# Two places for half sums in PSUM, another pattern of combined images from 126 to 145, and another order of the first steps, in a quantised 3x3 convolution after group normalisation

## The chip, the core and the metric

The kernel runs on one core of a Trainium2 chip. That core has five engines with a queue each, which run in order and meet only at semaphores: TensorE (PE, with its weight loads as PEld), VectorE (DVE), ScalarE (ACT), GpSimd (POOL), and SyncE (SP), which only issues DMAs here. Matmuls write to PSUM (8 banks of 128 partitions x 512 float32); DVE and ACT read it from there. The metric is the device time of one execution in microseconds; lower is better.

## What is computed

160 images of 128 channels and 32 x 32 pixels are normalised in groups of four channels, and convolved with 3x3 weights that are quantised to a two-part grid (a step s1 and a fifth of it, s2); the convolution is added to the image. Image i goes with weight set i // 32 of five in the kernel's order of images (the kernel takes the images set by set).

```python
def _L0_conv_ref(x, U):                    # N = 5 sets of weights, K = 3, PAD = 1
    beta = jnp.max(U)
    alpha = jnp.min(U)
    s1 = (beta - alpha) / 3.0
    v1 = s1 * floor(U / s1)
    s2 = s1 / 5.0
    v2 = s2 * floor((U - v1) / s2)
    w = (v1 + v2).reshape(OUT_CH * N, IN_CH, K, K)
    xb = x.reshape(B // N, N * C, H, W)
    act = conv_general_dilated(xb, w, strides 1, padding 1, feature_group_count=N)
    return act.reshape(B, C, H, W)
def _gn(v, G=32, eps=1e-5):                # mean and variance over (C // G, H, W)
    return (g - m) / jnp.sqrt(s + eps)
x = x + _L0_conv_ref(_gn(x), U)
```

## The kernel before

**Data.** Images are loaded two at a time into a ring of 11 places in SBUF (`load`), measured, normalised, convolved, added to and stored from there (`store`). The five sets of weights are quantised on DVE a column of the 3x3 taps at a time (`make_column`, some 13 DVE operations per column, handed out one by one by `take(later, 1)` between the images' work), turned by PE through PSUM (`turn_column`, tile `pt`) and kept by ACT and POOL (`keep_column`): for each column three taps (G), and three combinations of them for the half sums (SUM, DIFF, MINUS_G2).

**Statistics.** ACT reads each image twice (L194 sums, L201 squares); a few early images are measured by DVE instead (`BY_VECTOR`, with `bn_stats`, L184). For a group of 2, 4 or 8 images PE averages over channels (`means` L210, `variances` L227, tile `pg` in PSUM), ACT takes the result out (L219, L233), and POOL does the small arithmetic up to `rstd` and `shift` (L221 to L246). Groups end at images 2, 4, 8, 12, 16, 20, 24 and then every eight.

**Precision.** The normalised image is used as the sum of two float16 parts, high and low. An image that is not *combined* is normalised by ACT (`normalise`, z, L523), its high part cast by ACT (`high_part`, hi, L531), its low part made by DVE (`low_part`, lo, L589), and then combinations of the rows of lo alone by DVE (`combinations`, L603 to L606). Its high part goes through the nine taps directly (`taps`, L629: 18 matmuls of up to 512 columns); its low part goes through half sums.

**Half sums.** For a pair of output rows the vertical part of a 3x3 convolution is had from a sum and a difference of row pairs: PE makes m1 (SUM) and m2 (DIFF) of the half height in PSUM (`sums_of_pairs`), ACT copies m2 to SBUF (`leave`, L725), DVE writes m1+m2 and m1-m2 into the two banks of `eo` (`pairs`, L735 and L737), and PE adds the remaining terms into `eo` (`rest_of_column`). A *combined* image goes this way with both parts: POOL (`outer_rows`, L554, L555) and DVE (`combine`, L565 to L571) form the row combinations v of the raw image in float32, ACT scales and rounds them to vh (`high_combined`, L576), DVE makes vl (`low_combined`, L582). Before the change the odd images from 7 to 145 are combined, and from 146 on two of every three.

**Matmuls of an image.** Combined: 12 of 512 columns for the half sums and 24 of 256 in `rest_of_column`. Not combined: 6 of 512, 18 of 512 (taps) and 12 of 256.

**Order.** All is written out by hand in `run` (a manual schedule: each engine gets its instructions in the order of the program). In iteration i, `conv(i)` puts on PE the half sums of image i+1 and then the rest of image i; the other engines get, in this order: the low part of i+2; measuring, first half; taking image i-1 out of `eo` (`residual`: ACT L754 with a later adding DMA by POOL, L773; every eighth image, the first and the last ones by DVE, L765); the border rows of i+4; `leave(i+1)`; the high part of i+3; measuring, second half; `pairs(i+1)` on DVE; `combine(i+4)`, or a step of quantisation. The first three images are not combined and take both parts through the taps; image 2 uses the two banks of m1 and m2 as its output.

**PSUM.** Two `eo` of two banks each (`ps_eo`), one bank each for m1 and m2 (`ps_m`), one for the statistics (`ps_stat`), and one for turned weights and the range of the weights (`ps_tr`): eight.

Of the kernel before, what the change touches and what calls it, by code (L numbers as in the profile page):

```python
# [19 lines left out]
ROW = 3  # L20
# [139 lines left out]
class Statistics:  # L160
# [5 lines left out]
    def __init__(self, nc, small, psum, gavg, mhalf, nb, scale, name):  # L166
        self.nc, self.small, self.psum, self.gavg, self.mhalf = nc, small, psum, gavg, mhalf
        self.nb, self.scale, self.name = nb, scale, name

        self.mv = self.tile("mv", [nb, 2])  # L170
# [35 lines left out]
    def means(self):  # L206
        self.pg = self.psum.tile(
            [self.nc.NUM_PARTITIONS, 2, self.nb], F32, tag="pg", name=f"pg{self.name}"
        )
        self.nc.tensor.matmul(  # L210
            self.pg[:, 0, :], self.gavg, self.mv[:, :, 0], start=True, stop=True
        )
# [36 lines left out]
def general_path(tc, keep, steps, x, u, out):  # L249
# [8 lines left out]
    with tc.If(far > 0), ExitStack() as ctx:  # L258
# [9 lines left out]
        for n in range(N_SETS):  # L268
# [11 lines left out]
            with tc.For_i(0, IMGS // N_SETS, 1) as b:  # L280
                xt = one.tile([P, H * W], F32, tag="xt", name=f"g_xt{n}")
                nc.sync.dma_start(xt, xv[n, :, bass.ds(b, 1), :])
                stats = Statistics(nc, one, psum, gavg, mhalf, 1, 1.0, f"g{n}")
                stats.image(0, xt)
                stats.means()
# [26 lines left out]
class Main:  # L312
# [27 lines left out]
    BY_VECTOR = (8, 10, 11, 14, 19, 24, 29, 34)  # L340
    THIRDS = 146
# [7 lines left out]
    def __init__(self, tc, ctx, keep, x, u, out):  # L349
# [9 lines left out]
        def pool(name, bufs, **kw):  # L359
# [18 lines left out]
        self.ps_stat = pool("ps_stat", 1, space=PSUM)  # L378
        self.ps_tr = pool("ps_tr", 1, space=PSUM)
        self.steps = Steps(nc, keep)  # L380

        self.pair = [
            ps_m.tile([P, self.H // 2, self.W], F32, tag=name, name=name) for name in ("m1", "m2")
        ]
# [52 lines left out]
    def over_partitions(self, ext1, ident, between):  # L437


        nc, P = self.nc, self.P  # L440
        rows = self.ps_tr.tile([1, 2, P], F32, tag="pt", name="rows")
        for k in range(2):
            nc.tensor.transpose(rows[:, k, :], ext1[:, k : k + 1], ident)
        between()
        top = self.const.tile([1, 2], F32, tag="top", name="top")
        nc.vector.tensor_reduce(top, rows, AX.X, ALU.max)
        spread = self.ps_tr.tile([P, 2], F32, tag="pt", name="spread")
        nc.tensor.matmul(spread, self.ones, top, start=True, stop=True)
        return spread

    def make_column(self, n, col, by_scalar=False):

        nc, P = self.nc, self.P
        un = self.us[n].rearrange("o i (r c) -> o i r c", c=ROW)[:, :, :, col]
        k1, k2 = yield from self.steps.quantise(self.qpool, un, f"{n}_{col}", MM, by_scalar)
        if n == 0:
            parts = ((k1, self.ident5), (k2, self.ident))
            self.keep_column(n, col, self.turn_column(n, col, parts))  # L460
        else:
            m = self.qpool.tile([P, P, ROW], MM, tag="m", name=f"m{n}_{col}")
            nc.vector.scalar_tensor_tensor(m, k1, 5.0, k2, ALU.mult, ALU.add)
            self.columns.append((n, col, ((m, self.ident),)))
            yield

    def turn_column(self, n, col, parts):
        nc, P = self.nc, self.P
        pt = self.ps_tr.tile([P, ROW, P], F32, tag="pt", name=f"pt{n}_{col}")
# [6 lines left out]
        return pt  # L476

    def keep_column(self, n, col, pt):


        nc, P = self.nc, self.P
        wt = self.wpool.tile([P, 6, P], MM, tag=f"wt{col}", name=f"wt{n}_{col}")
        half = self.qpool.tile([P, ROW, P], MM, tag="half", name=f"half{n}_{col}")
        outer = self.qpool.tile([P, P], MM, tag="outer", name=f"outer{n}_{col}")
        nc.scalar.mul(wt[:, self.G, :], pt, 2.0 / LIFT)  # L485
        nc.scalar.mul(half, pt, 1.0 / LIFT)
# [4 lines left out]
        self.wts[n, col] = wt  # L491
# [5 lines left out]
    def stats_of(self, k):  # L497
        if k not in self.stats:
            self.stats[k] = Statistics(
                self.nc, self.small, self.ps_stat, self.gavg, self.mhalf, len(self.groups[k]),  # L500
                self.steps.lift, k,
            )
        return self.stats[k]
# [24 lines left out]

    def high_part(self, i):
# [4 lines left out]
    def combined(self, i):  # L534

        if i < self.STEADY or i >= self.imgs:
            return False

        return i % 2 == 1 if i < self.THIRDS else i % 3 != 1

# [135 lines left out]

    def both(self, i):
# [3 lines left out]
    def sums_of_pairs(self, i):  # L681

        both = self.both(i)
        for a, kind in ((1, self.DIFF), (0, self.SUM)):
            for col in self.COLS:
                for j, (_, st) in enumerate(both):
                    self.product(
                        self.pair[a], i, kind, st[:, a], col,
# [33 lines left out]
    def leave(self, i):  # L722

        m2 = self.evac.tile([self.P, self.H // 2, self.W], F32, tag="m2", name=f"m2_{i}")
        self.nc.scalar.copy(m2, self.pair[1])  # L725
        self.m2[i] = m2

    def pairs(self, i, between=lambda: None):
# [3 lines left out]
        m1, m2 = self.pair[0], self.m2.pop(i)  # L732
# [49 lines left out]
    def run(self):  # L782
# [44 lines left out]
        spread = self.over_partitions(ext1, ident, self.stats_of(0).means)  # L827
# [31 lines left out]
        self.stats[1].means()  # L859
# [8 lines left out]
        run(first)  # L868
        self.warm_up(2)
# [15 lines left out]
        run(second)  # L885
        measure(1, 5)
# [8 lines left out]
        self.stats[2].means()  # L895
        self.stats[2].deviations()
        self.low_part(3)
# [4 lines left out]
        for i in range(self.imgs):  # L902
# [3 lines left out]
            def on_the_way(col):  # L906
                if col == self.COLS[1]:
                    for st in ready:
                        st.means()
                    for *column, parts in self.columns:  # L910
                        turned.append((column, self.turn_column(*column, parts)))
# [32 lines left out]
            if i < self.FIRST:  # L944
# [5 lines left out]
                if i == 2:  # L950
# [4 lines left out]
                    self.pairs(3)  # L955
                    self.low_part(4)
                    run(self.combinations(4))
                self.residual(j)
                if i == 1:
                    measure(0, 11)  # L960
            else:
# [23 lines left out]
                if part:  # L985
                    self.normalise(i + 3)
# [11 lines left out]
            for column, pt in turned:  # L998
                self.keep_column(*column, pt)
            turned = []  # L1000

            if i >= self.FIRST:
# [5 lines left out]
                else:  # L1008
                    take(later, 1)
# [63 lines left out]
```

## Time and profile before

| | before |
|---|---|
| median of 4 runs (lowest to highest) | 991.56 us (991.36 to 991.73) |
| profiled execution: its own time | 991.84 us |
| its span, first to last instruction | 990.0 us |
| granted TensorE clock | 0.998 |

The page of the profile gives, for each engine, its busy time and share of the span, and the chain of work that ended last. Lines of a timeline give start (us from the span's start), duration, engine, source line, operation, output<-inputs, shape and how many in a row; in square brackets how long the engine was idle before and what ended that. Matmuls overlap in such lines (a row of 0.38 us is followed by the next start 0.216 us later), so PE's pace is read from starts, not from durations. Lines of waits give engine, line and tile, what it waited for, us in total, number and longest.

### The profile page before, as it was taken

What the parts mean: (1) busy time and instruction counts of PE and PEld (TensorE: products, weight loads), DVE (VectorE), ACT (ScalarE), POOL (GpSimd) and SP (SyncE); (2) the same over time, 40 slices, a digit from 0 to 9 for tenths busy, and PEclk for the clock granted to TensorE, in tenths of its full rate; (3) what the DMA queues carried; (4) which work ended last, traced back from release to release, by engine and by line L of the source; (5) the groups of instructions that cost most, each with busy time, mean ns of one, the idle gap of its engine ahead of it and who ended that gap; (6) DMA issues with size and microseconds to landing.
All of it is one profiled execution on the core that took longest, in us unless ns stands there. A gap on an engine that the chain in (4) does not pass through costs nothing.

```text
span 990.0 us, 16124 instructions
## 1 busy us (share of the span) xinstructions
PE 958.1 (97%) x5938; PEld 578.1 (58%) x5938; DVE 928.2 (94%) x1256; ACT 894.9 (90%) x1224; POOL 392.2 (40%) x565
## 2 busy tenths in 40 slices
PE   2899999999999999999999999999999999999997
PEld 1445665566656666666655666666665666666564
DVE  7999999999999999989999999999999998889995
ACT  5779999999999999999999999999999999998651
POOL 4424563643316253614363433315343424132410
PEclk9999999999999999999999999999999999999999
DMA  9538999999997999799989999997999898987764
GB/s 363 205 107 238 242 252 273 257 264 274 256 307 177 301 250 290 190 301 266 272 219 267 275 283 232 281 284 222 242 276 303 215 301 215 293 230 205 180 178 153
DMA packets 65129, 246.05 MB, mean 249 GB/s; under 512 B 5008, under 2 KB 5008, under 8 KB 65040
## 3 DMA queue, kind: packets, MB, share of 16 engines
q1 hardware_dynamic: 45312, 173.09, 50.2%
q0 software_dynamic: 19728, 71.84, 37.5%
q8 instruction: 48, 0.79, 0.3%
q14 instruction: 41, 0.34, 0.1%
HBM read 89.19 MB, written 83.89 MB: 175 GB/s over the span
## 4 chain that ended last, share of the span: by engine, by line
PE 70%; DVE 11%; ACT 9%; issue 4%; POOL 3%; DMA 2%; SPq 0%; DVEq 0%; ACTq 0%; POOLq 0%
PE eo L668 24%; PE m L668 23%; PE eo L629 23%; ACT junk L201 2%; ACT vh L576 2%; ACT sum L754 2%; DMA xt<-in_x_dram 1%; DVE eo L737 1%; DVE eo L735 1%; DVE lo L589 1%; POOL v L554 1%; DVE v L565 1%; ACT m L725 1%; POOL rstd L237 1%; ACT z L523 1%
## 5 line engine op out<-in xcount | busy, mean ns | idle before, releaser
L668 PEld LDWEIGHTS <-wt 128*128 128x128 f16 x4266 | 417.2, 98 | 235.6 <-issue 7.6
L629 PE MATMUL eo<-hi,wt 128*128 128x496 f16 (+3 forms) x1422 | 339.6, 375 | 1.2 <-ACT wt L485 0.7
L773 POOL DMA_DIRECT2D xt<-sum x137 | 122.6, 903 | 457.1 <-ACT sum L754 442.5
L629 PEld LDWEIGHTS <-wt 128*128 128x128 f16 x1494 | 146.0, 99 | 141.8 <-ACT wt L485 2.1
L582 DVE SCALAR_TENSOR_TENSOR vl<-v,rstd,vh 128x2048 f16<-128x2048 f32 x80 | 188.1, 2351 | 4.4 <-ACT vh L576 4.4
L668 PE MATMUL m<-vh,wt 128*128 128x496 f16 (+1 forms) x480 | 182.2, 380 | 2.0 <-DVE eo L737 1.2
L668 PE MATMUL eo<-vl,wt 128*128 128x248 f16 (+1 forms) x960 | 183.9, 273 | 0.0
L668 PE MATMUL eo<-vh,wt 128*128 128x248 f16 (+1 forms) x960 | 183.9, 273 | 0.0
L668 PE MATMUL m<-vl,wt 128*128 128x496 f16 (+1 forms) x480 | 182.2, 380 | 0.2 <-DVE vl L582 0.2
L194 ACT ACTIVATE junk<-xt 128x1024 f16<-128x1024 f32 x152 | 160.6, 1057 | 16.1 <-DMA xt<-in_x_dram 12.2
L201 ACT ACTIVATE junk<-xt,mv 128x1024 f16<-128x1024 f32 x152 | 173.8, 1143 | 0.1
L576 ACT ACTIVATE vh<-v,rstd 128x2048 f16<-128x2048 f32 x80 | 160.8, 2010 | 2.5 <-POOL v L555 2.0
L754 ACT ACTIVATE sum<-eo 128x1024 f32<-128x1024 f32 x137 | 138.0, 1007 | 14.9 <-PE eo L668 14.8
L735 DVE TENSOR_TENSOR eo<-m,m 128x512 f32<-128x512 f32 x157 | 109.0, 695 | 35.6 <-ACT m L725 28.9
L668 PE MATMUL eo<-rows,wt 128*128 128x256 f16 (+1 forms) x924 | 138.9, 273 | 0.0
L668 PE MATMUL m<-rows,wt 128*128 128x496 f16 (+1 forms) x462 | 113.6, 380 | 0.7 <-DVE eo L737 0.3
L737 DVE TENSOR_TENSOR eo<-m,m 128x512 f32<-128x512 f32 x157 | 109.4, 697 | 3.6
L725 ACT COPY m<-m 128x512 f32<-128x512 f32 x157 | 90.5, 577 | 18.4 <-PE m L668 18.4
L523 ACT ACTIVATE z<-xt,shift,rstd 128x1024 f32<-128x1024 f32 x80 | 99.8, 1248 | 2.7 <-POOL shift L244 2.6
L589 DVE TENSOR_TENSOR lo<-z,hi 128x1024 f16<-128x1024 f32 x80 | 97.8, 1223 | 0.0
L565 DVE TENSOR_TENSOR v<-xt 128x960 f32<-128x960 f32 x80 | 91.8, 1147 | 0.0
L531 ACT CAST hi<-z 128x1024 f16<-128x1024 f32 x80 | 83.6, 1045 | 2.5
(111 smaller groups left out, 895.6 us busy)
## 6 DMA issues: line engine op xcount, KB each, us to landing
xt<-in_x_dram SPq DMA_DIRECT2D x78, 1024.0 KB, 9.2
out_dram<-xt SPq DMA_DIRECT2D x78, 1024.0 KB, 5.8
xt<-sum POOLq DMA_DIRECT2D x137, 512.0 KB, 6.4
u<-in_L_conv_U_dram SPq DMA_DIRECT2D x4, 576.0 KB, 9.2
xt<-in_x_dram SPq DMA_DIRECT2D x4, 512.0 KB, 9.2
range<-in_L_conv_U_dram SPq DMA_DIRECT2D x3, 576.0 KB, 7.3
out_dram<-xt SPq DMA_DIRECT2D x3, 512.0 KB, 2.9
u<-in_L_conv_U_dram SPq DMA_DIRECT2D x2, 288.0 KB, 2.9
```

Of the source, the lines that this page charges most:

```text
L194: self.nc.scalar.activation(junk, image, ACTF.Copy, scale=-1.0 / image.shape[1], accum_out=self.mv[:, j, 0:1],)
L201: self.nc.scalar.activation(junk, image, ACTF.Square, bias=self.mv[:, j, 0:1], accum_out=self.mv[:, j, 1:2],)
L523: nc.scalar.activation(z, self.image(i), ACTF.Identity, bias=st.shift[:, j : j + 1], scale=st.rstd[:, j : j + 1],)
L576: self.nc.scalar.mul(vh, self.v[i], st.rstd[:, j])
L582: self.nc.vector.scalar_tensor_tensor(vl, self.v[i], st.rstd[:, j], self.hi[i], ALU.mult, ALU.subtract)
L589: self.nc.vector.tensor_sub(lo[:, 1 : self.H + 1, :].rearrange("p h w -> p (h w)"), self.z.pop(i), self.hi[i].rearrange("p h w -> p (h w)"),)
L629: nc.tensor.matmul(self.bank(target, h)[:, r0 - h0 : r1 - h0, c0:c1], self.wts[n, col][:, k, :], tile[:, s0 : s0 + r1 - r0, c0 + dw : c1 + ...
L668: self.nc.tensor.matmul(target[:, :, c0:c1], self.wts[n, col][:, kind, :], source[:, :, c0 + dw : c1 + dw], start=start, stop=stop, skip_g ...
L735: nc.vector.tensor_add(rows[:, :, 0], m1, m2)
L737: nc.vector.tensor_sub(rows[:, :, 1], m1, m2)
L754: nc.scalar.mul(self.sum[i], eo.rearrange("p h r w -> p (h r w)"), 0.5)
L773: self.nc.gpsimd.dma_start(self.image(i), self.sum.pop(i), accum_op=ALU.add)
```

## The change

Five things change. (1) m1 has two places, `m1a` for even and `m1b` for odd images. To free the bank for it, the statistics (`pg`) and the turned weights (`pt`) share one bank as fixed parts of one tile; the rows of the weight range and the means of the first two groups are put in the two `eo` places, which are not in use then. (2) Of the images 126 to 145, those at places 0, 2 and 4 of each five are combined, twelve in place of ten. (3) Of the others, those at place 3 (129, 134, 139; 144 begins a group and is left out) are normalised by DVE at the end of the iteration before ACT would have done it. (4) For the third column of the first weights, what `keep_column` did is split: taps, then the means, then halves, the deviations, and the sums of the halves on POOL behind the deviations. (5) Image 11 is measured (by DVE) behind `pairs(3)` in iteration 2, not at the end of iteration 1.

```diff
@@ Statistics
-    def means(self):
-        self.pg = self.psum.tile(
-            [self.nc.NUM_PARTITIONS, 2, self.nb], F32, tag="pg", name=f"pg{self.name}"
-        )
+    def means(self, place):
+        self.pg = place[:, : 2 * self.nb].rearrange("p (k j) -> p k j", k=2)
@@ Main.__init__
+    FIFTHS = 126
     THIRDS = 146
...
-        self.ps_stat = pool("ps_stat", 1, space=PSUM)
-        self.ps_tr = pool("ps_tr", 1, space=PSUM)
+        ps_small = pool("ps_small", 1, space=PSUM)
...
-        self.pair = [
-            ps_m.tile([P, self.H // 2, self.W], F32, tag=name, name=name) for name in ("m1", "m2")
-        ]
+        self.m1a, self.m1b, self.m2_ps = (
+            ps_m.tile([P, self.H // 2, self.W], F32, tag=name, name=name)
+            for name in ("m1a", "m1b", "m2")
+        )
+        self.pair = [self.m1a, self.m2_ps]
+        small = ps_small.tile([P, 512], F32, tag="small", name="small")
+        self.pt, self.pg = small[:, : ROW * P].rearrange("p (k o) -> p k o", k=ROW), small[:, ROW * P :]
@@ over_partitions
-        rows = self.ps_tr.tile([1, 2, P], F32, tag="pt", name="rows")
+        place = self.bank_pair("range").rearrange("p h r w -> p h (r w)")
+        rows = place[0:1, 0, : 2 * P].rearrange("p (k c) -> p k c", k=2)
...
-        spread = self.ps_tr.tile([P, 2], F32, tag="pt", name="spread")
+        spread = place[:, 1, :2]
@@ keep_column
+    def keep_taps(self, n, col):
+        P = self.P
+        wt = self.wpool.tile([P, 6, P], MM, tag=f"wt{col}", name=f"wt{n}_{col}")
+        self.nc.scalar.mul(wt[:, self.G, :], self.pt, 2.0 / LIFT)
+        self.wts[n, col] = wt
+    def keep_halves(self, n, col):
+        half = self.qpool.tile([self.P, ROW, self.P], MM, tag="half", name=f"half{n}_{col}")
+        self.nc.scalar.mul(half, self.pt, 1.0 / LIFT)
+        return half
+    def keep_sums(self, n, col, half):
...
+    def keep_column(self, n, col):
+        self.keep_taps(n, col)
+        self.keep_sums(n, col, self.keep_halves(n, col))
@@ normalise
+    def normalise_by_vector(self, i):
+        st, j = self.column_of(i)
+        z = self.z[i] = self.zpool.tile([self.P, 1024], F32, tag="z", name=f"z{i}")
+        self.nc.vector.tensor_scalar(
+            z, self.image(i), st.rstd[:, j], st.shift[:, j], ALU.mult, ALU.add
+        )
@@ combined
-        return i % 2 == 1 if i < self.THIRDS else i % 3 != 1
+        if i < self.FIFTHS:
+            return i % 2 == 1
+        return (i - self.FIFTHS) % 5 % 2 == 0 if i < self.THIRDS else i % 3 != 1
+    def by_vector_too(self, i):
+        if not self.FIFTHS <= i < self.THIRDS or (i - self.FIFTHS) % 5 != 3:
+            return False
+        return i != self.groups[self.group_of[i]].start
@@ sums_of_pairs, pairs
+    def m1(self, i):
+        return self.m1b if i % 2 else self.m1a
...
-                        self.pair[a], i, kind, st[:, a], col,
+                        self.m2_ps if a else self.m1(i), i, kind, st[:, a], col,
...
-        m1, m2 = self.pair[0], self.m2.pop(i)
+        m1, m2 = self.m1(i), self.m2.pop(i)
@@ run, ahead of the loop
-        self.stats[2].means()
+        self.keep_taps(0, self.COLS[2])
+        self.stats[2].means(self.pg)
+        half = self.keep_halves(0, self.COLS[2])
         self.stats[2].deviations()
+        self.keep_sums(0, self.COLS[2], half)
@@ run, iterations 1 and 2
                     self.pairs(3)
+                    measure(0, 11)
                     self.low_part(4)
                     run(self.combinations(4))
                 self.residual(j)
-                if i == 1:
-                    measure(0, 11)
@@ run, later iterations
                 if part:
-                    self.normalise(i + 3)
+                    if not self.by_vector_too(i + 3):
+                        self.normalise(i + 3)
                     self.high_part(i + 3)
...
                 if self.combined(i + 4):
                     self.combine(i + 4)
                 else:
+                    if self.by_vector_too(i + 4):
+                        self.normalise_by_vector(i + 4)
                     take(later, 1)
```

## The prediction

> **What bounds the kernel now.** I read the page's busy shares and its chain of waits first, then the busy time by stretch, then PE's own timeline start by start.
>
> ```profile
> PE 958.1 (97%) x5938; PEld 578.1 (58%) x5938; DVE 928.2 (94%) x1256; ACT 894.9 (90%) x1224; POOL 392.2 (40%) x565
> ...
> PE 70%; DVE 11%; ACT 9%; issue 4%; POOL 3%; DMA 2%; SPq 0%; DVEq 0%; ACTq 0%; POOLq 0%
> ```
>
> PE holds 70% of the chain, but DVE and ACT stand close behind. In stretches (the change's images 126 to 145 are roughly 771 to 888 us; columns: us, busy time of PE, PEld, DVE, ACT, POOL):
>
> ```profile
> 56.00:230.00 174.00, 171.14 (x1047) 101.13 (x1046) 168.93 (x247) 164.49 (x231) 86.43 (x112) 1.00 0.90 243
> 230.00:770.00 540.00, 539.62 (x3379) 328.53 (x3378) 517.49 (x685) 521.95 (x718) 214.30 (x294) 1.00 0.93 262
> 771.00:888.00 117.00, 117.00 (x733) 71.31 (x732) 104.61 (x131) 113.88 (x156) 40.00 (x68) 1.00 0.91 250
> ```
>
> Up to 230 us DVE is as full as PE (5 us idle of 174); from 771 to 888 DVE has 12.4 us to spare, ACT only 3.1. A busy PE can still hide a lost third of a microsecond, because its rows overlap; so starts are what I count. A plain piece, images 124 to 126:
>
> ```profile
> 777.22 0.38 PE L668 MATMUL m<-vh,wt 128*128 128x512 f16 x1
> ...
> 779.81 1.43 PE L629 MATMUL eo<-hi,wt 128*128 128x512 f16 x6
> ...
> 784.94 1.46 PE L668 MATMUL m<-rows,wt 128*128 128x512 f16 x6
> 786.23 0.38 PE L668 MATMUL eo<-vh,wt 128*128 128x256 f16 x2
> ...
> 789.03 0.38 PE L668 MATMUL m<-vh,wt 128*128 128x512 f16 x1
> ```
>
> Half sums of a combined image take 779.81-777.22 = 2.59 us and its rest 789.03-786.23 = 2.80, less 0.17 for the three turns of weights in between: 5.22. An image that is not combined takes 786.23-784.94 = 1.29 and 784.94-779.81 = 5.13: 6.42. A stall at m1 looks like this:
>
> ```profile
> 478.63 0.81 PE L668 MATMUL m<-rows,wt 128*128 128x512 f16 x3
> 479.75 0.81 PE L668 MATMUL m<-rows,wt 128*128 128x512 f16 x3 [0.30 <-DVE eo L737]
> 480.39 0.38 PE L668 MATMUL eo<-vh,wt 128*128 128x256 f16 x2
> ```
>
> Three matmuls at 0.216 end at 479.28; the next starts at 479.75, because m1 is still being read at L737. 0.47 us lost.
>
> **More images combined.** In 126 to 145 ten are combined now; the new pattern (places 0, 2, 4 of each five) makes twelve. PE: 2 x (6.42-5.22) = 2.40 us less, in a stretch where PE never stands still. The cover is DVE and ACT keeping up. DVE, by spacings of starts: a combined image costs 1.06+0.67+0.60 (L565, L568, L571) and 2.27 (L582) = 4.60; another 1.13+0.60+0.34+0.34 = 2.41. So +4.4 us for two. ACT: vh 1.91 instead of z 1.28 and hi 0.95, -0.6 for two. POOL gets two more pairs of border rows (L554, L555), 1.0+0.8 us each, within 77 us idle; its adding DMAs (L773, 0.9 us each) stand behind them, and a store behind those, with nothing due sooner than four images on.
>
> **z by DVE.** Places 3 are 129, 134, 139 and 144; 144 begins a group, so three. ACT loses 3 x 1.28 = 3.8 us. The trace has no such row on DVE. Nearest: L101, a tensor_scalar of 384 elements, starts 0.33 apart; L112, a scalar_tensor_tensor of 384, 0.53, and L582 with 2048, 2.27, that is 1.04 ns an element and 0.13 fixed. At that slope 1024 elements are 1.20 us; with L101's (0.33-0.13)/384 they are 0.66. I take 0.66, since L101 is the same operation: +2.0, at most +3.6. DVE's sum is +6.4 to +8.0 against 12.4 spare; over any five images 13.8+4.8+0.7 and five times 1.3 for the pair sums make 25.8 of PE's 28.5. It is queued behind pairs(i+1) and ahead of the next vl, so vl waits for it. At the first doubles (125, 126) DVE has no gap until 795.7. Walking its queue by these spacings: vl(126) is done at 782.1 and needed at 784.9; rows(127) 789.3, needed 790.3; vl(128) 793.6 to 794.1, needed 794.3. It fits, but with 0.2 to 0.7 left, and PE arrives earlier by what it has gained. The one double in the trace (145 to 147, at 916.7) lost 0.32 waiting for vl. I put +0.3 for all four doubles; bounds 0 and 4 x 0.32 = 1.3.
>
> **Two places for m1.** The half sums of image i+1 no longer wait until pairs(i) has read m1; PE now meets that wait at the first eo matmul of L629/L668, three matmuls (0.65) or six (1.30) later. Every PE instruction is queued behind it either way. After 230 us the lost starts of this kind are 0.19 (338), 0.47 (479), 0.19 (526), 0.19 (714), 0.05 (762), 0.26 (918) and 0.04 (952): 1.39, each below its cover, and there DVE and ACT are not full. All 1.39 gained. m2 stays single: its evacuation is not touched. Before 230 us the m1 waits sum to 2.9 (largest 0.80 at 151.7 and 0.75 at 188.4), but DVE is full, and the chain runs through vh on ACT and border rows on POOL, not through PE; only the last, 0.26 at 225, is surely free.
>
> **The beginning.** Moving dv ahead of the weight sums on POOL (four rows from 48.98 to 50.76) would end PE's wait at 51.9 earlier; but turned weights and means now share a bank, and program order puts the means (PE at 47.71) behind the first read of the weights (ACT, 48.05 to 48.5). PE's next tap matmuls go 0.28 later, ngm 0.5 later, so 0.47 of the 0.76 is left. Image 11's measuring on DVE (56.02 to 57.70) goes behind pairs(3): eo of image 3 comes some 0.65 earlier (the 0.67 stall at 58.3 ends), but DVE then waits 1.4 for m2, and its 1.7 us come in front of lo(4): rows(4) ends near 62.5 instead of 61.66, and DVE, full until 89, is 0.9 late. The two cancel. No DMA is issued in the pieces that move, so SP's queue keeps its order. For everything ahead of 230 us I take -0.3. Bounds: all m1 waits, the 0.67 and the 0.47 gained, -4.0; or one more starved POOL operation, as at 176, after which PE lost 0.61 and 0.75: +1.4.
>
> ```profile
> 175.99 5.32 POOL L554 TENSOR_SCALAR v<-xt,ngm 128x32 f32<-128x32 f32 x1
> ```
>
> While DVE runs L565 to L606 without a break, this border row of 0.3 us takes 5.3. [...]
>
> Range and places in the rest of the change (rows of the weight range in an eo bank, first means beside them): both banks are read out at 24.3 and 26.1, ahead of eo's first use in image 0 (28.85) and image 1 (about 30): nothing. If that cover went, PE would wait there by as much.
>
> **Sum.** -2.40 - 1.39 - 0.3 + 0.3 = -3.8. The profiled execution is 991.84, span 990.0 and 1.84 around it; 988.05. It lies 0.28 over the median of 991.56, so 987.8.
>
> **Rivals.** (1) ACT is the true pace: only 3.1 us idle of 117, so PE's gain is given back as waits for vh or m2. For it: DVE waits 8.1 us for m2 copies there. Against: ACT loses 4.4 us of work in just these images, more than PE's 2.4; and its rare idle time ends on PE:
>
> ```profile
> ACT ngm L219 <- PE pg L210: 1.8, 2, 0.9
> ACT sum L754 <- PE eo L668: 0.5, 1, 0.5
> ```
>
> Then only the 0.5 that ACT itself waited for PE at L754 comes off: 991.1.
> (2) m1's waits only move to eo or vl, as DVE and not the place was late. For it: the stall at 479 follows L765, a DVE residual. Against: the covers. Then 2.4-0.3 are left: 989.5.
> (3) Slower: at doubles two vl and two combines follow each other, DVE runs from vl to vl with z between, POOL's border rows starve as at 176, vh comes late, and PE loses 0.61+0.75 = 1.36 at a double. It decides from three doubles of four (4.1, more than the 3.8 gained); with all four and one more before 230, 6.8-3.8: 994.5. For it: the 5.3 us row. Against: L554 averages 1.0, and in 771 to 888 DVE pauses for PSUM work every 5 us.
>
> **Numbers.** Forecast 0.66, rival 1 0.07, rival 2 0.17, rival 3 0.10. Range 985.0 to 990.6: below, 2.8 more of the early waits; above, rival 2 with 1.1 at the doubles. Under 0.2% (2.0 us) a measurement can't tell from no change. Faster: forecast and most of rival 2, 0.80; same 0.11; slower 0.09.
>
> **What would show it.** PE starts 5.22 apart for twelve images and 6.42 for eight; no gap between the third and fourth m<-rows after 230 us; a DVE z row of 0.66 to 0.75 us; ACT idle from 126 to 145 above 3.1; at 51 to 66 us PE's stalls gone but rows(4) later. Wrong would be: waits for vl or vh of over 0.3 at each double, or PE later than before at 230.

## The result and the profile after

The changed kernel takes 990.04 us (median of 40 runs, 988.79 to 991.99), the kernel before in the runs beside it 991.71 (60 runs, 991.24 to 993.47): a ratio of 0.9984, 95% interval 0.9980 to 0.9989. It is faster by 1.7 us. The forecast was 3.8, so the sign and the kind of gain were right and 2.1 us of it did not come. The time lies inside the stated range of 985.0 to 990.6, but near its upper end, and nearer to the 989.5 of rival 2 than to the 987.8 of the forecast. The profiled execution took 990.91 us, its span 989.2.

Its busy shares and chain, as on the page:

```profile
PE 957.2 (97%) x5938; PEld 578.5 (58%) x5938; DVE 934.3 (94%) x1259; ACT 891.7 (90%) x1219; POOL 406.6 (41%) x569
...
PE 66%; DVE 13%; ACT 12%; issue 5%; POOL 2%; DMA 1%; SPq 0%; DVEq 0%; ACTq 0%; POOLq 0%
```

PE holds 66% of the chain instead of 70%, DVE 13% instead of 11% and ACT 12% instead of 9%: a little more of the chain now lies with DVE and ACT. The same three stretches (columns: us, busy time of PE, PEld, DVE, ACT, POOL, then clock, DMA share, GB/s):

```profile
56.00:230.00 174.00, 170.87 (x1046) 100.68 (x1045) 168.52 (x246) 164.53 (x232) 84.60 (x112) 1.00 0.89 241
230.00:770.00 540.00, 540.00 (x3384) 329.04 (x3382) 518.48 (x686) 523.35 (x719) 220.54 (x296) 1.00 0.94 263
771.00:888.00 117.00, 115.78 (x736) 71.39 (x735) 110.93 (x135) 110.43 (x151) 50.23 (x72) 1.00 0.93 251
```

From 230 to 770 us PE now has no idle moment. From 771 to 888 it has 1.2 us, which it did not have before, although ACT's idle time there rose from 3.1 to 6.6 us: what PE waits for must be DVE, whose busy time rose from 104.6 to 110.9. PE's timeline at the first double (images 125 and 126, both combined) shows it; columns are start, duration, engine, line, operation, and in brackets the idle time and its releaser:

```profile
776.90 0.38 PE L699 MATMUL m<-vh,wt 128*128 128x512 f16 x1
777.78 0.38 PE L699 MATMUL m<-vl,wt 128*128 128x512 f16 x1 [0.50 <-DVE vl L613]
...
780.15 1.43 PE L660 MATMUL eo<-hi,wt 128*128 128x512 f16 x6
```

Two neighbours start 0.88 apart where 0.22 is the rule: 0.66 us lost, and the half sums of image 125 take 780.15-776.90 = 3.25 us instead of 2.59. DVE's queue says why:

```profile
772.45 0.70 DVE L771 TENSOR_TENSOR eo<-m1b,m 128x512 f32<-128x512 f32 x1
773.05 1.15 DVE L596 TENSOR_TENSOR v<-xt 128x960 f32<-128x960 f32 x1
774.12 0.74 DVE L599 SCALAR_TENSOR_TENSOR v<-xt,twice 128x512 f32<-128x512 f32 x1
774.78 0.68 DVE L602 TENSOR_TENSOR v<-xt 128x512 f32<-128x512 f32 x1
775.38 2.35 DVE L613 SCALAR_TENSOR_TENSOR vl<-v,rstd,vh 128x2048 f16<-128x2048 f32 x1
```

The three rows L596 to L602 combine image 126. They stand ahead of L613, the vl of image 125, without a gap; vl is done at 777.73, and PE wanted it at 777.12. In the kernel before, nothing of image 126 stood there; DVE's row and PE's row were

```profile
773.46 2.34 DVE L582 SCALAR_TENSOR_TENSOR vl<-v,rstd,vh 128x2048 f16<-128x2048 f32 x1
...
777.44 0.38 PE L668 MATMUL m<-vl,wt 128*128 128x512 f16 x1
```

so vl was done at 775.80, 1.64 us before PE wanted it. Now it ends 1.93 later and is wanted 0.32 earlier, which uses up the 1.64 and 0.61 more.

To set the kernels side by side, those of the experiments below included, one row each: the start of the first half sum matmul (m<-) of an image, minus the start of the same one in the profile before, in us. One execution each; "clock" is the granted clock from 40 to 44 us, which turns out to matter.

| kernel | clock 40-44 | image 3 | 5 | 24 | 32 | 125 | 126 | 146 | last matmul |
|---|---|---|---|---|---|---|---|---|---|
| changed | 0.57 | +0.63 | +1.96 | +1.15 | +0.75 | -0.32 | +0.34 | -0.69 | -0.99 |
| changed, again | 1.00 | -0.38 | +0.93 | +0.17 | -0.24 | -1.31 | -1.21 | -2.42 | -2.73 |
| image 11 put back | 1.00 | -0.35 | -0.34 | -1.15 | -0.85 | -1.92 | -1.78 | -2.74 | -3.05 |
| sums put back | 1.00 | +0.79 | +1.56 | +0.83 | +0.44 | -0.63 | -0.49 | -1.71 | -2.01 |
| both put back | 1.00 | +0.87 | +0.87 | +0.08 | +0.39 | -0.68 | -0.25 | -1.26 | -1.56 |
| one place for m1 | 1.00 | -0.24 | +1.08 | +1.44 | +1.46 | +1.77 | +2.70 | +2.38 | +2.40 |
| odd pattern | 0.61 | +0.24 | +1.58 | +0.79 | +1.10 | +0.03 | +0.03 | +0.03 | -0.26 |
| m1 alone | 1.00 | +0.76 | +0.76 | -0.07 | -0.48 | -1.54 | -1.54 | -1.54 | -1.85 |
| z by ACT | 1.00 | -0.41 | +0.91 | +0.15 | +0.44 | -0.63 | -0.06 | -1.85 | -2.15 |
| image 11 back, z by ACT | 0.61 | +0.24 | +0.26 | -0.55 | -0.95 | -2.02 | -1.27 | -3.05 | -3.35 |
| image 11 back, odd pattern | 0.60 | +0.28 | +0.30 | -0.50 | -0.21 | -1.28 | -1.28 | -1.28 | -1.58 |
| image 11 back, two of three | 1.00 | -0.43 | -0.41 | -1.24 | -1.64 | -2.71 | -2.52 | (147) -4.11 | -4.73 |
| vl first | 0.59 | +0.32 | +1.64 | +0.91 | +1.21 | +0.15 | +0.15 | +3.07 | +3.11 |

Two executions of the changed kernel differ by 1.7 us at the last matmul: 1.0 of it is there at image 3, the rest comes at the doubles. A single profile can't settle a change of 1.7 us. The differences within a row, from one image to a later one, are steadier and are what is used below: the twelve profiles of kernels with two places for m1 all gain 0.73 to 0.83 from image 5 to 24, and 1.06 or 1.07 from 32 to 125. Only from 24 to 32 do they fall into two kinds, whatever the kernel: six gain 0.4, six lose 0.3. What parts these no run shows.

### The profile page after: what moved, and what is told of

It reads as the page before. It is cut to its first block, busy times and chain, and to the rows that moved or that the text cites. A ratio compares the mean times of both kernels' runs of the same rounds, so it can differ in the third digit from the quotient of the medians.

```text
span 989.2 us, 16124 instructions
## 1 busy us (share of the span) xinstructions
PE 957.2 (97%) x5938; PEld 578.5 (58%) x5938; DVE 934.3 (94%) x1259; ACT 891.7 (90%) x1219; POOL 406.6 (41%) x569
## 4 chain that ended last, share of the span: by engine, by line
PE 66%; DVE 13%; ACT 12%; issue 5%; POOL 2%; DMA 1%; SPq 0%; DVEq 0%; ACTq 0%; POOLq 0%
PE eo L699 22%; PE eo L660 21%; PE m L699 11%; PE m1b L699 7%; PE m1a L699 4%; ACT junk L201 3%; ACT vh L607 3%; ACT sum L788 2%; DVE v L596 2%; ACT m L759 1%; DVE eo L769 1%; DVE eo L771 1%; DVE lo L620 1%; ACT z L538 1%; DVE vl L613 1%
## 5 line engine op out<-in xcount | busy, mean ns | idle before, releaser
L660 PE MATMUL eo<-hi,wt 128*128 128x496 f16 (+3 forms) x1386 | 332.1, 376 | 1.6 <-ACT wt L487 0.9
L613 DVE SCALAR_TENSOR_TENSOR vl<-v,rstd,vh 128x2048 f16<-128x2048 f32 x82 | 192.9, 2353 | 1.1 <-ACT vh L607 1.1
L699 PE MATMUL eo<-vh,wt 128*128 128x248 f16 (+1 forms) x984 | 188.5, 273 | 0.0
L699 PE MATMUL eo<-vl,wt 128*128 128x248 f16 (+1 forms) x984 | 188.5, 273 | 0.0
L538 ACT ACTIVATE z<-xt,shift,rstd 128x1024 f32<-128x1024 f32 x75 | 93.6, 1248 | 3.2 <-POOL shift L243 3.2
L699 PE MATMUL m<-vl,wt 128*128 128x496 f16 (+1 forms) x246 | 93.4, 380 | 1.8 <-DVE vl L613 1.7
L596 DVE TENSOR_TENSOR v<-xt 128x960 f32<-128x960 f32 x82 | 94.1, 1147 | 0.0
L699 PE MATMUL m<-vh,wt 128*128 128x496 f16 (+1 forms) x246 | 93.4, 380 | 0.3 <-ACT m L759 0.3
L585 POOL TENSOR_SCALAR v<-xt,ngm 128x32 f32<-128x32 f32 x82 | 83.7, 1021 | 0.1
L699 PE MATMUL m1b<-vh,wt 128*128 128x496 f16 (+1 forms) x213 | 80.9, 380 | 0.0
L699 PE MATMUL m1b<-vl,wt 128*128 128x496 f16 (+1 forms) x213 | 80.9, 380 | 0.0
```

The costliest lines, as they stand in the source:

```text
L538: nc.scalar.activation(z, self.image(i), ACTF.Identity, bias=st.shift[:, j : j + 1], scale=st.rstd[:, j : j + 1],)
L596: nc.vector.tensor_sub(v[:, W:last], x[:, : last - W], x[:, 2 * W :])
L613: self.nc.vector.scalar_tensor_tensor(vl, self.v[i], st.rstd[:, j], self.hi[i], ALU.mult, ALU.subtract)
L660: nc.tensor.matmul(self.bank(target, h)[:, r0 - h0 : r1 - h0, c0:c1], self.wts[n, col][:, k, :], tile[:, s0 : s0 + r1 - r0, c0 + dw : c1 + ...
L699: self.nc.tensor.matmul(target[:, :, c0:c1], self.wts[n, col][:, kind, :], source[:, :, c0 + dw : c1 + dw], start=start, stop=stop, skip_g ...
```

## The experiments

All were timed against the kernel before in runs beside them. Two groups of four ran beside a kernel before of 991.87 us, the first below (vl first, odd pattern, both put back, one place) beside 992.14; so ratios are compared across groups, and medians within one. The expectations of the first four are in us beside a kernel before of 991.71; 0.4 us is to be taken off their medians to hold them against these. Edits are against the changed kernel.

| kernel | median us | ratio to before, 95% |
|---|---|---|
| vl first | 993.76 | 1.0017 (1.0008 to 1.0026) |
| odd pattern | 990.97 | 0.9987 (0.9978 to 0.9996) |
| both put back | 989.81 | 0.9975 (0.9966 to 0.9984) |
| one place for m1 | 993.54 | 1.0014 (1.0005 to 1.0023) |
| changed, again | 990.10 | 0.9984 (0.9975 to 0.9993) |
| image 11 put back | 988.60 | 0.9964 (0.9952 to 0.9976) |
| z by ACT | 989.23 | 0.9973 (0.9962 to 0.9984) |
| m1 alone | 990.29 | 0.9984 (0.9975 to 0.9993) |
| sums put back | 990.77 | 0.9989 (0.9980 to 0.9998) |
| image 11 back, z by ACT | 987.61 | 0.9958 (0.9944 to 0.9972) |
| image 11 back, odd pattern | 989.66 | 0.9977 (0.9968 to 0.9986) |
| image 11 back, two of three | 988.63 | 0.9967 (0.9955 to 0.9979) |

**vl first.** At the doubles, vl of the first image is queued on DVE ahead of the combining of the second.

```diff
                 if self.combined(i + 2):
-                    self.low_combined(i + 2)
+                    if not self.early_low(i + 2):
+                        self.low_combined(i + 2)
...
+                if self.early_low(i + 3):
+                    self.low_combined(i + 3)
                 if self.combined(i + 4):
                     self.combine(i + 4)
```

> The changed kernel (990.0 us), but at a double (two combined images one after the other: 125/126, 130/131, 135/136, 140/141) the first one's vl goes on VectorE ahead of the second one's row combinations. Theory (the order at the doubles makes vl late): PE's waits for vl near 777, 806 and 836 us (0.66, 0.46, 0.40 in the changed kernel's trace) go, 1.0 to 1.5 us faster, about 988.7. Rival (VectorE is short over the whole stretch): the waits only move to eo or to vh, under 0.4 us faster.

A clear miss: 3.3 thousandths slower than the changed kernel. PE did not wait for vl of image 125 any more, but the wait went to ACT, which needs the combined v of image 126. The waits of this kernel from 771 to 888 us (engine, line, releaser: total us, times, longest):

```profile
ACT vh L610 <- DVE v L605: 7.8, 4, 3.2
DVE eo L772 <- ACT m L762: 7.3, 6, 1.3
```

and ACT's timeline at the first double:

```profile
778.06 2.00 ACT L610 ACTIVATE vh<-v,rstd 128x2048 f16<-128x2048 f32 x1 [2.22 <-DVE v L605]
```

In the changed kernel these two waits are 2.1 us each. vh comes 2 us late, all that is queued behind it on ACT (the copy of m2 too) is late, and DVE then waits for m2. Neither of these two orders of DVE's queue is in time for both PE and ACT; other orders were not tried. Less work in front is tried below (z by ACT).

**Odd pattern.** Odd images are combined from 126 to 145 as before, and no z goes to DVE; the rest is as changed.

```diff
-        return (i - self.FIFTHS) % 5 % 2 == 0 if i < self.THIRDS else i % 3 != 1
+        return i % 2 == 1 if i < self.THIRDS else i % 3 != 1
```

> The changed kernel with the odd images combined from 126 to 145 as before and no z by VectorE; two places for m1 and the new beginning stay. Theory (the doubles give back 2.0 of the 2.4 us): only 0.2 to 0.6 us slower than the changed kernel, 990.2 to 990.6. Rival (the profiled execution showed more waits than most and the pattern is worth its 2.4): 992.2 to 992.6, slower than before.

0.3 thousandths above the changed kernel, well inside the intervals; 990.5 on the scale of the expectation, in the theory's range. In this profile PE stands at +0.03 at every image from 124 to 148, and the view of PE's waits from 771 to 888 us is empty. All the loss at the doubles belongs to the new pattern.

**Both put back.** Image 11's measuring and the order of the weight sums as in the kernel before.

```diff
                     self.pairs(3)
-                    measure(0, 11)
                     self.low_part(4)
...
                 self.residual(j)
+                if i == 1:
+                    measure(0, 11)
...
-        self.stats[2].deviations()
         self.keep_sums(0, self.COLS[2], half)
+        self.stats[2].deviations()
```

> The changed kernel with image 11 measured at the end of iteration 1 and the third column's sums of weights on GpSimd ahead of the deviations, both as before; PSUM as changed. Theory (the new order of the beginning makes rows(4) and rows(5) late: 0.58 and 0.64 us of new waits at 63 and 67 us): 1.0 to 1.5 us faster than the changed kernel, 988.5 to 989.0. Rival (the late start was the arrival of the weights, which varies): within 0.3 us of it.

0.9 thousandths better than the changed kernel by the ratios, 0.7 us by the medians on the scale of the expectation: less than the theory's least, and two to three times the rival's most. The intervals overlap, so this run alone says only that the new beginning probably costs something as a whole. Its two parts are split below.

**One place for m1.** Every image uses m1a.

```diff
-        return self.m1b if i % 2 else self.m1a
+        return self.m1a
```

> The changed kernel with one place for m1 (m1a for every image). Theory (each wait at m1 that lies under its cover is a gain): the waits after 230 us come back (1.1 to 1.4 us), and up to 1.2 more ahead of 230: 991.1 to 992.6. Rival (m1's waits only move): within 0.4 us of 990.0.

More than the theory: 3.0 thousandths slower than the changed kernel, and slower than the kernel before. PE's timeline at the stall that the prediction showed, first in the changed kernel, then here:

```profile
479.19 0.81 PE L699 MATMUL m<-rows,wt 128*128 128x512 f16 x3
479.84 0.81 PE L699 MATMUL m1a<-rows,wt 128*128 128x512 f16 x3
480.49 0.38 PE L699 MATMUL eo<-vh,wt 128*128 128x256 f16 x2
```

```profile
480.10 0.81 PE L699 MATMUL m<-rows,wt 128*128 128x512 f16 x3
481.38 0.81 PE L699 MATMUL m1a<-rows,wt 128*128 128x512 f16 x3 [0.47 <-DVE eo L771]
```

0.65 from m to m1 is three matmuls at 0.216; with one place it is 1.28. The starts lost at m1 are 1.39 us from 230 to 771, 0.27 at 920, and 2.35 at the doubles (0.66, 1.24, 0.18 and 0.27). The forecast priced the place by the stalls of the old pattern alone; the new pattern would have made more of them. With one place the new pattern loses 0.6 us from image 125 to 146 in this profile, where with two places it gains 0.4 to 1.2.

**The changed kernel again**, beside the next three.

> The changed kernel itself once more, beside the others on one chip, so that they can be held against it directly. Both theories: 0.998 to 0.9989 of the kernel before, about 1.6 us below it. It also shows how far PE's starts vary from one profiled execution to the next: the starts of the half sums of image 5 should again be 1.0 to 2.0 us later than before's.

0.9984 as the first time; image 5 at +0.93, just outside the expected 1.0 to 2.0, from an execution that was 1.0 us earlier at image 3.

**Image 11 put back.** The first two parts of the diff of "both put back".

> Only the measuring of image 11 is put back to the end of iteration 1; the new order of the weight sums stays. Theory (image 11's 1.69 us of DVE rows ahead of lo(4) are what makes rows(4) and rows(5) late; where they stood before, DVE was idle anyway, 1.63 us before pairs(3)): PE's waits for rows(4) and rows(5) go, the half sums of image 5 start 1.0 to 1.3 us earlier than in the changed kernel, and 0.4 to 0.9 us of it are left in the time, as much as with both parts put back (the run before gave about 0.9). Rival (the deviation that ends 1.2 us later, so that z of image 4 and the copy of m2 come late, is what counts): image 5 less than 0.4 us earlier, time within 0.3 us of the changed kernel.

The waits for rows(4) and rows(5) are gone and image 5 starts 1.27 us earlier than in the changed kernel of the same clock. The time falls by 2.0 thousandths, 1.5 us by the medians, more than the theory; the intervals of the two just touch. PE's starts give the size: at image 24, in profiles of the same clock, the kernels with the measuring moved stand at +0.17 and +0.15 (changed again, z by ACT) and those with it put back at -1.15 and -1.24 (this one, two of three). So the 1.3 us of image 5 are all still there at image 24. DVE's timeline of the changed kernel (first profile),

```profile
58.36 0.70 DVE L769 TENSOR_TENSOR eo<-m1b,m 128x512 f32<-128x512 f32 x1 [1.63 <-ACT m L759]
59.09 0.70 DVE L771 TENSOR_TENSOR eo<-m1b,m 128x512 f32<-128x512 f32 x1
59.70 1.28 DVE L184 BATCH_NORM_STATS2 st<-xt 128x6 f32<-128x512 f32 x2
...
61.39 1.22 DVE L620 TENSOR_TENSOR lo<-z,hi 128x1024 f16<-128x1024 f32 x1
```

PE's waits in the same profile, of which the first, for eo of image 3, is there in the kernel before too and the two for rows(4) and rows(5) come of the move,

```profile
59.85 1.44 PE L660 MATMUL eo<-hi,wt 128*128 128x512 f16 x6 [0.54 <-DVE eo L771]
...
64.06 0.82 PE L699 MATMUL m<-rows,wt 128*128 128x512 f16 x3 [0.42 <-DVE rows L637]
...
67.72 0.82 PE L699 MATMUL m<-rows,wt 128*128 128x512 f16 x3 [0.48 <-DVE rows L637]
```

and DVE's with image 11 put back:

```profile
55.67 1.28 DVE L184 BATCH_NORM_STATS2 st<-xt 128x6 f32<-128x512 f32 x2
...
57.36 0.70 DVE L769 TENSOR_TENSOR eo<-m1b,m 128x512 f32<-128x512 f32 x1
58.09 0.70 DVE L771 TENSOR_TENSOR eo<-m1b,m 128x512 f32<-128x512 f32 x1
58.70 1.22 DVE L620 TENSOR_TENSOR lo<-z,hi 128x1024 f16<-128x1024 f32 x1
```

In its old place the measuring fills the hole in which DVE waits for the copy of m2 anyway, and lo(4) follows the pair sums at once. In the new place the hole stays open (1.63 us) and the 1.69 us stand ahead of lo(4).

**z by ACT.** No image's z goes to DVE; three of five are still combined.

```diff
-        if not self.FIFTHS <= i < self.THIRDS or (i - self.FIFTHS) % 5 != 3:
-            return False
-
-        return i != self.groups[self.group_of[i]].start
+        return False
```

> The three normalisations that the change gave to DVE are given back to ACT; the pattern of three combined in five stays. Theory (DVE is what is late at the doubles; its queue has no idle time from z of image 129 at 791.2 us to the vl of image 130 at 804.5, so z's 0.92 us lie in front of that vl; ACT has 6.6 us to spare there and 3.8 of it go): the waits of 0.46 us for vl of image 130 and of 0.40 for vl of image 135 shrink or go, the first double (125 and 126, with no z before it) keeps its 0.66, and the kernel is 0.4 to 1.2 us faster than the changed one. Rival (ACT sets the pace as soon as more images are combined, which is why z went to DVE): waits for m2 or vh in place of these, 0.5 us or more slower than the changed kernel.

0.9 us faster than the changed kernel beside it, as the theory had it; the intervals overlap, but the place agrees. PE's lost starts from 125 to 145, from the table's method: with z on DVE (changed, first profile) 0.66 at image 125, 0.79 at 130 (vl and then eo), 0.19 at 132 and 0.39 at 135; with z by ACT 0.57, nothing, 0.19 and 0.42. The loss at image 125, where no z stands in front yet, differs from execution to execution: 0.10 to 0.75 in the seven profiles with three combined in five and two places (vl first left aside). From image 126 on they part cleanly: until image 146 the five with z on DVE gain 0.96 to 1.22 us on the kernel before, the two with z by ACT 1.78 and 1.79. So z on DVE costs 0.6 to 0.8 us. The vl of image 130 in DVE's queue, changed kernel:

```profile
791.21 1.00 DVE L547 TENSOR_SCALAR z<-xt,rstd,shift 128x1024 f32<-128x1024 f32 x1
792.13 2.51 DVE L613 SCALAR_TENSOR_TENSOR vl<-v,rstd,vh 128x2048 f16<-128x2048 f32 x1
...
804.51 2.35 DVE L613 SCALAR_TENSOR_TENSOR vl<-v,rstd,vh 128x2048 f16<-128x2048 f32 x1
```

and with z by ACT:

```profile
803.27 2.34 DVE L610 SCALAR_TENSOR_TENSOR vl<-v,rstd,vh 128x2048 f16<-128x2048 f32 x1
```

In the changed kernel DVE runs from 785 to 807 us without idling, so z's 0.92 us (start to start) reach the next double: vl ends at 806.86 where PE wanted it at 806.45, against 805.61 and 806.04 with z by ACT. The wait at 135, expected to shrink too, did not. And ACT took z without becoming the pace: it is busy for 114.16 us of 117, and the view of waits names only vl for PE in the stretch.

**m1 alone.** The edits of "both put back" and "odd pattern" together: of the change only the places in PSUM are left.

> The two places for m1 and the shared bank alone: image 11's measuring, the order of the weight sums and the odd images combined from 126 to 145 as in the kernel before. Theory (the parts add: the run with one place lost about 3.0 us against the changed kernel, the pattern is worth 0.3 to 0.6, and the old beginning gives 0.9): 990.2 to 990.6 where the kernel before is 992.1, which is 1.5 to 1.9 us faster than before and about as fast as the whole change. Rival (the places pay only where images are combined two in a row and in the new beginning): within 0.5 us of the kernel before.

0.9984, the same as the whole change, as the theory said. New beginning and new pattern together brought nothing that the intervals could show.

**Sums put back.** The last part of the diff of "both put back", alone.

> Only the order of the weight sums on POOL is put back ahead of the deviations; image 11 is measured where the change put it. It completes the four cases of the beginning: both new 0.9984 of the kernel before, image 11 back 0.9964, both back 0.9975. Theory (the two parts add: image 11's move costs 2.0 us, the new order of the sums gains 1.1): about 0.9995, 1.1 us slower than the changed kernel, with the waits for rows(4) and rows(5) still there and one wait of some 0.7 us for dv on POOL back. Rival (image 11's move only costs because the deviations end later, so either part put back mends it): about 0.997, 1 us faster than the changed kernel.

0.9989; the rival's 0.997 is outside the interval, the theory's 0.9995 inside. Image 11's move costs with the old order of the sums too: at image 24 PE stands at +0.83, where the two profiles with both put back (both put back, m1 alone) have +0.08 and -0.07. The wait for dv on POOL is back (1.01 us before L226 in the profile), and image 3 starts 1.17 us later than in the changed kernel of the same clock.

**Image 11 back, z by ACT.** The candidate: both edits together.

> Image 11's measuring put back and z given back to ACT, all else as changed: the candidate that should beat both kernels. Theory (they stand in stretches that do not touch; the first gave 1.5 us against the changed kernel on one chip, the second 0.9): 0.9955 of the kernel before, about 987.7 where that is 991.9, 2.2 to 2.6 us below the changed kernel. Rival (the gain of z by ACT was only its profile's earlier arrival in the stretch, and an earlier PE meets DVE's backlog at the doubles): no better than image 11 alone, 0.9964.

987.61 us, 0.9958 (0.9944 to 0.9972): the lowest median of all, 4.3 us below the kernel before, and its interval lies clear of the changed kernel's. Both gains are in its profile: PE stands at -0.55 at image 24, where the three profiles with the new beginning and the same low clock (0.57 to 0.61) have +0.79 to +1.15, and 1.78 us are gained from image 126 to 146. Against image 11 put back alone the median is 1.0 us lower, with intervals that overlap.

**Image 11 back, odd pattern**, the run beside it without the new pattern.

> Image 11's measuring put back, two places for m1, and odd images combined from 126 to 145 as before (no z by DVE): the run beside it without the new pattern. Theory (the pattern gives 0.4 to 1.1 of its 2.40 us and loses the rest to waits for vl at the doubles): 0.9967 to 0.9975, 0.4 to 1.1 us slower than image 11 put back alone, and PE without a wait from 126 to 145. Rival (once the beginning is mended the pattern gives nothing): as fast as image 11 put back alone, within 0.2 us.

0.9977. The new pattern with z by ACT is worth 1.9 thousandths against it by the medians, 1.03 us by PE's starts from image 125 to 146 (1.22 in the other profile with z by ACT); with z on DVE 1.3 thousandths, and by the starts of five profiles (0.37, 0.58, 0.82, 1.08 and 1.11) 0.8 us. The theory's 0.4 to 1.1 fits the starts.

**Image 11 back, two of three.** THIRDS is 126, z by ACT: thirteen of the twenty images combined.

> As the candidate, but from image 126 on two of three images are combined, as the kernel does from 146: 13 of the twenty instead of 12, seven doubles instead of four, z by ACT. Theory (a double costs 0.3 to 0.5 us of lateness of vl, because DVE has no idle time there): 1.2 us less work of PE, 0.9 to 1.5 more lost at three further doubles: within 0.5 us of the candidate. Rival (the loss is one of DVE's sum, which two of three raises by another 2.2 us, so that it falls behind from double to double): 1 us or more slower than the candidate.

988.63 us, 0.9967 (0.9955 to 0.9979), 1.0 us over the candidate, with intervals that overlap. In its profile PE gains 1.40 us from image 125 to 147 against the candidate's 1.03, with one wait of 1.6 us for vl. Undecided between the two expectations.

## Why the forecast came too high

The sum on record was -2.40 - 1.39 - 0.3 + 0.3. The two profiles of the changed kernel, averaged, give by stretch: +0.26 up to image 32, -1.07 from there to 125, -0.74 from 125 to 146, -0.30 at the end, together -1.86. Of the 1.9 us that are missing against the sum, 1.4 are missing from 125 to 146 and 0.6 up to image 32; the rest came as forecast.

**Two places for m1: right.** -1.39 was forecast after 230 us, which is from image 32 on. All twelve profiles with two places gain 1.06 or 1.07 from image 32 to 125, and ten of them 0.29 to 0.31 after 146, so 1.37 in all. The m1 stalls return as 1.39 before 771 us and 0.27 at 920 with one place (before they were 1.09 and 0.30), and in the changed kernel no start is lost at m1. Alone the places bring 1.6 us, the whole net gain of the change. Rival 2 (the waits only move) falls by this, although its time was the nearer one. Ahead of 230 us the forecast called only 0.26 us of these waits surely free; the twelve profiles gain 0.73 to 0.83 from image 5 to 24, where the kernel with one place loses 0.36. That this gain was left out and hid part of what the beginning cost is luck.

**More images combined: the saving was right, the term "+0.3 for all four doubles" was mis-sized.** It measured 1.3 to 2.0 us (2.40 less the 1.11 and 0.37 of the two profiles; 2.03 in the first by the four places above). The step that failed is the walk through DVE's queue: it followed vl(126), rows(127) and vl(128), and found 0.2 to 0.7 us left, but left out vl(125), which stands behind the combining of 126 and is the first to be needed. PE waited right there, 0.66 and 0.10 us in the two profiles. The rest was lost at the doubles for which the forecast made no walk: 0.79 and 0.61 at image 130, where z stands in front as well, and 0.19 and 0.40 at 132 and 135; the fourth double lost nothing. That stretch's sum (25.8 of 28.5 us in five images) was no comfort: the spare time lies elsewhere in the five. The four doubles were taken as alike, and are not.

**z by DVE: too low in price, wrong in place.** The three rows took 803, 806 and 1003 ns, the first of them 0.92 us from start to start; 0.66 was taken, 1.20 was the bound.

```profile
L547 DVE TENSOR_SCALAR z<-xt,rstd,shift x3: 803/806/1003, 791.2 to 848.3; 128x1024 f32<-128x1024 f32 x3
```

The forecast held that it fits. It costs 0.6 to 0.8 us, at image 130, and brings ACT an idleness that nobody needs. No border row of POOL ran beside one of these three z rows (the nearest ended at 847.38, ahead of the z at 848.30), so what a z on DVE does to one was not shown.

**The beginning: -0.3 forecast, +0.75 and -0.24 in the two profiles.** These two numbers mix the beginning with what the second place gains between image 5 and 32. At image 5, in the profile of full clock, PE is 0.93 late, and the runs give the parts. Sharing a bank costs 0.76 (m1 alone, at image 3 and 5): there the means stand behind ACT's first read of the turned weights, as the prediction said, first the kernel before, then m1 alone,

```profile
47.71 0.28 PE L210 MATMUL pg<-mv,gavg 128*128 128x4 f32 x2
```

```profile
48.69 0.39 PE L209 MATMUL small<-mv,gavg 128*128 128x4 f32 x2 [0.71 <-ACT wt L487]
```

The new order of the sums wins back 1.17 and 1.22 at image 3 (changed again against sums put back, image 11 put back against both put back). Of the dv wait of 0.76 the forecast kept 0.47 as gain after this cost; at full clock PE is 0.24 to 0.43 earlier at image 3, a little less. The step that failed is image 11's move. It was said to cancel out: the stall of 0.67 at eo of image 3 would end, and DVE would be "0.9 late" at rows(4). The stall did not end (0.71 and 0.69 in the two profiles, the first at 59.85 above), since DVE only waits longer for m2, and PE lost 0.58 and 0.64 more at rows(4) and rows(5). The move cost 1.3 us, all of it still there at image 24. What DVE lost in front of lo(4) was not made good; DVE is nearly full until 230 us (168.5 us of 174).

**The signs on record.** ACT's idle time from 771 to 888 us (6.6), the late rows(4) and the missing stalls at m1 came as forecast; the z row was longer. Of the signs of being wrong, a wait for vl of over 0.3 us came at three doubles of four in the first profile (0.66, 0.46, 0.40) and at one in the second (0.40), and PE was late near 230 us in the first (+0.75) and not in the second (-0.24).

**The other rivals.** ACT as the true pace (rival 1) falls with z by ACT: 3.7 us more work on it, and the kernel is faster. Rival 3 saw the right place and the wrong path. Its starved border rows do not appear: the only wait for them in that stretch is 0.2 us,

```profile
ACT vh L607 <- POOL v L586: 0.2, 1, 0.2
```

and the doubles cost 2 us through vl, not 4 through vh. The kernel with one place does end slower than before, but through m1.

## What to carry to other kernels

When two heavy items follow each other on an in-order engine, walk its queue for every consumer from the item before the pair on, not only for the new ones; a sum over the stretch hides it. Work that is moved is worth what the hole it leaves was worth: see whether the engine was idle there anyway, and whether the new place has something queued behind it that the bound engine needs. And a change of several parts should be split: here one part alone brought as much as the whole, and with two edits put back the gain of 1.7 us became 4.3.

## Something not expected: the clock after a short stall

At 37 to 40 us PE waits 2.0 to 2.8 us in two pieces for quantised weights. In some profiles it comes back at full pace, in others not. The first profile of the changed kernel from 36 us on (columns as above; the clock is the third number from the right):

```profile
36.00:40.00 4.00, 2.51 (x16) 1.11 (x14) 3.72 (x8) 1.03 (x3) 0.00 (x0) 1.00 0.07 26
40.00:44.00 4.00, 3.71 (x10) 1.42 (x11) 3.72 (x7) 3.97 (x7) 3.00 (x4) 0.57 0.01 4
```

and the second:

```profile
40.00:44.00 4.00, 4.00 (x20) 1.84 (x21) 3.69 (x7) 3.97 (x6) 3.02 (x4) 1.00 0.12 13
```

In the first profile matmuls of 496 columns start 0.42 to 0.43 us apart from 40.52 to 43.85 us, instead of 0.216. Five of the thirteen profiles of kernels after the change have 0.57 to 0.61 there, eight 1.00, and that part of the code was not touched between them. It costs some 0.7 us: with the new order of the sums image 3 starts 0.24 to 0.63 late in the cases of low clock and 0.24 to 0.43 early in the others.

The traces show more of it. PE's first matmuls of 512 columns start 0.427 us apart, and 0.216 from one moment on, which lies at 23.67 to 26.89 us in the fourteen profiles (24.43 in the kernel before, 26.86 in the first profile of the changed kernel). In the five cases of low clock the granted clock is at half for 3.41 us each time, and this begins 13.65 us (the first profile of the changed kernel, 26.86 to 40.52) or 17.07 us (the other four) after that moment: four or five times 3.41. PE is not idle for the whole 3.41 us ahead of the half clock: counted at 0.216 us for 512 columns, its matmuls fill 0.99 to 1.26 us of them (1.26 in the first profile, from 37.10 to 40.52). Of every other such piece, counted from that moment on and up to 960 us, they fill 1.34 us or more in the fourteen profiles (at least 1.89 in the kernel before). An estimate from these fills, which all fourteen agree with: a piece that is filled for less than about 1.3 of its 3.41 us is followed by one at half the clock, and how full it is hangs on the length of the two stalls and on where the pieces fall on them. It is an agreement and not an experiment, for no run moved the pieces, and the gap between 1.26 and 1.34 is small.
